# Query scales moved from the weights to the evictions, and one column tile size, in a four-layer cross-attention kernel

## The chip, the cores and the metric

The kernel runs on one core of one Trainium2 chip. The metric is device time in microseconds of one execution, the median of several runs. The time before is 1969.5 us (3 runs, 1969.37 to 1971.12).

## The reference

For each of 16 batches, queries x (100 x 256) pass through four cross-attention layers against one context (361 x 256); everything is float32. Cut to what matters:

```python
# layer 0: 16 heads of 16, layer norm of queries and of context, then a feed-forward part
qn, kn, vn = ln(x, ln1_g, ln1_b), ln(ctx, ln1_g, ln1_b), ln(ctx, ln1_g, ln1_b)
x = x + attention(qn @ wq + bq, kn @ wk + bk, vn @ wv + bv) @ wo + bo
x = x + gelu(ln(x, ln2_g, ln2_b) @ w1 + b1) @ w2 + b2
# layer 1: 16 heads of 64, RMS norm of queries, context as it is
x = x + attention((rms(x) * norm_w) @ wq, ctx @ wk, ctx @ wv) @ wo
# layer 2: 16 heads of 64, rotary embedding of q and k, mask, residual, layer norm behind
x = ln(x + attention(rope(x @ Wq), rope(ctx @ Wk), ctx @ Wv, mask) @ Wo, ln_gamma, ln_beta)
# layer 3: 16 heads of 16, layer norm of queries (gq, betaq) and of context (gkv, betakv)
x = x + attention(ln(x, gq, betaq) @ Wq + bq, ..., ...) @ Wo + bo
```

A norm with scale g and shift b ahead of a product can be written in two ways: (z*g + b) @ W + bias, or z @ (g*W) + (b @ W + bias), with z the normalized rows.

## The kernel before

**Staging.** All weights stay in SBUF, in 12 slabs of 1 MB each (128 x 2048). Slab 0 holds the four weights of layer 0, slab 11 those of layer 3; the others hold one weight each. One SP queue issues the transfers in a fixed chain: inputs of batch 0, column vectors, slab 0, constants, mask of batch 0, inputs of batch 1, row vectors, slabs 1 to 11. The raw context of a batch has one buffer (ctxr).

**Folding.** fold() (L487) takes a scale and a shift into weights. shift (L502) is a TensorE product of the weight with the shift, matmuls with one column of moving data; add_bias (L512) adds the bias and gives a column in `folded`; scale (L527) multiplies the rows of the weight on VectorE or GpSimd. For values, the bias goes on through the output weight into a row (L551, L557). Before the change this is done for wk, wq and wv of layer 0, for w1, and for Wq, Wk and Wv of layer 3; for wq of layer 1 only the scale.

**A batch.** keys_T transposes the context twice, raw (cT) and normalized (zT). queries_T (L650) transposes normalized queries z by four TensorE transposes (L664) into two PSUM banks, and each bank is copied to xT by ScalarE or VectorE (copied, L604 and L606). It is called five times per batch, three times for normalized queries with a folded scale and shift (layer 0, feed-forward, layer 3). project_T and on_columns (L708) do the projections. Attention works in units of four heads: scores (L815), for layer 2 the mask (L860), the maximum (L863), exp (L866), reciprocal (L838), division by the sum on GpSimd (L845), transposes of the probabilities (L899), their copies (pT), and the weighted values (L935). Residuals run through project_out and project_out_T (L1007).

**Tile modes.** TensorE's array is used in tiles. Scores of 64 rows and transposes are "row64", scores of 16-wide heads are "row32", projections take column tiles of 64 ("col64") or 32 ("col32"), whichever is set (ANY_COLUMNS). Weighted values take col64 for heads of 64 and col32 for heads of 16. The folding has no mode (None).

**Order.** Nothing is issued in the order in which the program is written. Each piece of work goes into a Plan with its engines, expected costs, buffers and mode. Plan.order (L208) simulates the engines and picks the next piece: among those whose inputs and buffers are given, the one that starts first, then that of lowest rank. The rank comes from the batch, the length of the chain behind the piece, and ORDER's numbers for each batch ("batch", "lag") and each place in a batch ("place"). Leaving a tile mode counts as late by "keep" nanoseconds until the mode has run for "run". "pull" counts work of the other mode that is at hand:

```python
if engine == "PE" and start < free_at["PE"] + ORDER["window"]:
    m = mode if set_now else w.modes[0]
    at_hand[m] = at_hand.get(m, 0.0) + busy
```

Buffers named with p = b % 2 are separate for even and odd batches, so about two batches are in work at a time.

Of the kernel before, what the change touches and what calls it, by code (L numbers as in the profile page):

```python
# [17 lines left out]
P = 128  # L18
# [13 lines left out]
for _name, _w in (  # L32
# [12 lines left out]
    ("L0_xattn_wq", "L0_xattn_wk", "L0_xattn_wv", "L0_xattn_wo"),  # L45
# [10 lines left out]
    "lag": 38400, "pull": 0.05, "window": 0,  # L56
    "keep": {None: 890, "row64": 230, "row32": 260, "col64": 340, "col32": 1300},
    "run": {None: 2660, "row64": 8610, "row32": 9590, "col64": 0, "col32": 580},
    "batch": (-18000, 5000, 3000, 2500, 0, -3500, -2000, -500, 4000, 500, -500, -1500, -1500, 1500, 2000, -30500),
    "place": [  # L60
        100 * k for k in (
        -449, 380, -410, -907, -297, -381, -841, -547, -865, -451, -58, -715, -384, -1275, -204,
        -641, 28, -182, 1370, -396, -764, -381, 852, -627, -112, 190, -9, -445, -3, -270, -165,
        -33, -304, -1025, -413, 303, 189, 748, 664, 428, 334, -443, 389, -680, 26, 45, -389,
        -703, -298, -815, 382, 144, -234, -178, -319, -57, -490, 535, -270, -557, 24, 37, -252,
        -893, -744, -709, -7, -615, -499, -843, -1740, -583, -894, -541, 9, -686, -216, -11,
        -752, 14, -65, -104, -468, 267, 152, -304, 178, -1193, -774, -328, -678, -328, 230, 62,
        -355, -400, -649, -377, -283, 67, -55, 958, -172, 913, 10, -206, -336, -713, -315, -919,
        -196, -1027, -1062, 110, -555, 199, -65, 638, -159, -330, -421, -1032, -459, -215, -509,
        -581, 677, -93, -54, -2, -397, -37, -164, 39, -112, 653, -319, -353, 304, -753, -267,  # L70
        -601, -483, -215, 631, -145, -379, -439, -89, -73, -773, 104, -225, 235, -417, 26, -258,
        13, -847, -1259, -285, -870, 806, -187, -611, 97, 247, -582, -680, 50, -1341, -248, -93,
        -616, -282, -235, -362, -155, 207, 94, 84, 80, -312, 78, -97, -754, -266, 199, -192,
        -730, -101, -622, -421, -44, 28, 272, 825, 35, 688, -974, -421, 99, -655, -589, -47,
        -596, -713, -247, -457, -229, 16, -8, -207, 57, 717, 105, -410, -430, -320, -80, -938,
        -425, -769, -201, -686, -203, -784, -115, -998, -715, -1135, -1148, -736, -659, -883,
        -423, -884, -340, -196, -208, -45, 21, -200, -443, -268, 144, -548, -442, 252, -63, 450,
        0, 579, -46, 20, 860, 146, -344, -813, -172, -250, 576, -43, -365, -496, -37, -48, 63,
        -524, 157, -854, 1077, 547, -55, 635, -106, 360, -340, 719, -224, -240, -384, 434, 98,
        -620, -34, 307, 467, 169, -533, -297, 357, -181, 345, 49, -249, -145, 132, 86, -613,  # L80
        -65, -229, -858, 50, 445, -116, 64, -92, 11, 52, 185, 242, 201, 148, -390, -231, -174,
        -101, 39, -360, -62, 745, 81, 97, -526, -14, 324, -4, 136, 120, 442, -331, 163, -56,
        -176, -297, 608, 379, 66, -125, 660, 278, 251, -61, 531, 319, 711, 828, -180, -66, 279,
        -14, -193, -319, -511, -66, -29, 83, 113, 31, -672, -659, -715, -95, -394, -632, 260,
        -250, 170, -179, -139, -14, 37, -407, -1281, -867, -1330, -1460, -919, -876, -673,
        -2528, -934, -1119, -766, -1231, -576, -595, -612, -708, -115, 489, 492, 25, 2, 709,
        682, 185, 91, 381, -723, 578, 713, 883, -107, 47, -29, 470, -264, -587, 294, -539, 205,
        511, 423, 312, 1194, 30, 288, 344, -534, 37, -29, -165, -729, -641, -757, -867, -180,
        -1043, -773, -2062, -647, -1793, -1205, -894, -1713, -2979, -1137, 480, -214, -732,
        -916, -495, -1134, 349, -519, 213, -1447, -683, 961, -1008, -1158, -424, -1113, -152,  # L90
        -394, -88, 120, -537, 445, -938, 43, -331, -1264, -1001, -589, -634, -395, -837, -386,
        -399, -199, -576, -704, -569, -1503, -1874, -612, -1400, 35, -689, 192, 101, -184, 648,
        -1555, 146, -563, -45, -17, -467, -239, 338, -101, -408, 321, 31, 300, 37, -514, -472,
        131, -1083, -709, 337, -131, -233, -1021, -499, -1152, -521, -555, -660, 1181, -1469,
        -901, -1632, -540, -1293, 38, 0, 355, 184, 358, 379, 123, -235, -102, 603, -537, -68,
        -207, 39, -451, -373, 620, 695, 238, -360, 624, -675, -500, -309, 228, -1657, -1006,
        -1864, -2116, -1377, -1805, -1217, -2242, -2683, -3027,
# [208 lines left out]
def tile_xattn_layers(  # L306
# [112 lines left out]
    def load_slab(i):  # L419
        t = const.tile([P, 2048], F32, name=f"slab{i}")  # L420
        b = load_const(t, slabs[i], 2.6, f"slab{i}")
        names = SLABS[i]
        n = len(names)
        for k, name in enumerate(names):
            part = t[:, k * (2048 // n) : (k + 1) * (2048 // n)]
            kc = 8 if n == 1 and name[-2:].lower() in ("wo", "w2") else 2
            w[name] = part.rearrange("p (c n) -> p c n", c=kc)
            slab_of[name] = b
# [11 lines left out]
    load_slab(0)  # L440
    cst_b = load_const(cst, consts, 1.0, "cst")
    plan.batch = 0
    masks[0] = load_mask(0)
    plan.batch = 1
    loads[1] = load_inputs(1, 1000.0, 5000.0)
    plan.batch = -1
    rows_b = load_const(rows, rowvecs.partition_broadcast(P), 1.7, "rows")
    for i in range(1, len(SLABS)):
        load_slab(i)
# [34 lines left out]
    folded = const.tile([P, 7, 8], F32, name="folded")  # L484
    fold_at, ready_w = {}, {}

    def fold(slab_names, g, b, outs):  # L487

        src = slab_of[slab_names[0]]
# [28 lines left out]
        if biased:  # L518
            n = sum(w[o[0]].shape[2] // P for o in biased)
            plan.add(on_pe((1, 4 * n)), shift, reads=[src, colt_b], writes=[ps])  # L520
            plan.add(on_dve(8, len(biased)), add_bias, reads=[ps, colt_b], writes=[fb])
        for name, _, out_bias in outs:
            ready_w[name] = plan.buf(None, f"ready_{name}")

            def scale(eng, name=name):
# [7 lines left out]
                on_dve(n, 2) + on_pool(2 * n * 1.5), scale, reads=[src, fb, colt_b],  # L533
# [3 lines left out]
            if out_bias is not None:  # L537
# [22 lines left out]
                plan.add(on_pe((E, 4)), through, reads=[wide, src], writes=[rps])  # L560
# [9 lines left out]
        [("L0_xattn_wk", "L0_xattn_bk", None), ("L0_xattn_wq", "L0_xattn_bq", None),  # L570
# [3 lines left out]
    def fold_later():  # L574
        fold_b["ff"] = fold(
            SLABS[1], "L0_xattn_ln2_g", "L0_xattn_ln2_b", [("L0_xattn_w1", "L0_xattn_b1", None)]
        )
        fold(SLABS[3], "L1_xattn_norm_w", None, [("L1_xattn_wq", None, None)])

        fold_b["3q"] = fold(  # L580
            SLABS[11], "L3_xattn_gq", "L3_xattn_betaq", [("L3_xattn_Wq", "L3_xattn_bq", None)]
        )
        fold_b["3k"] = fold(
# [63 lines left out]
    def whole(a):  # L647
        return a

    def queries_T(src, p, name, cls="xT"):  # L650


        t = plan.buf(f"{cls}{p}", name)
# [718 lines left out]
```

## Time and profile before

| | |
|---|---|
| median of 3 runs | 1969.5 us |
| profiled execution | 1972.8 us, span 1971.0 us |
| mean granted TensorE clock | 0.991 |
| TensorE busy | 1932.3 us, 98% |
| VectorE, ScalarE, GpSimd busy | 1383.9, 1113.1, 954.6 us |
| TensorE matmul instructions | 30809 |
| one-column matmuls of the folding (L502) | 80 instructions, 13.2 us busy |
| period of one batch in the steady state | 119.5 us |

A float32 matmul of the program is two matmul instructions in the trace, each with its weight load. A shape such as 128*64 128x512 is rows * columns of the tile, then the moving data. Busy times of TensorE overlap, since matmuls are pipelined and tiles run side by side; the time from the start of one group to the start of the next is the time that the group costs. A batch's period is read from groups that come back in the same order.

### The profile page before, as it was taken

What the parts mean: (1) busy time and instruction counts of PE and PEld (TensorE: products, weight loads), DVE (VectorE), ACT (ScalarE), POOL (GpSimd) and SP (SyncE); (2) the same over time, 40 slices, a digit from 0 to 9 for tenths busy, and PEclk for the clock granted to TensorE, in tenths of its full rate; (3) what the DMA queues carried; (4) which work ended last, traced back from release to release, by engine and by line L of the source; (5) the groups of instructions that cost most, each with busy time, mean ns of one, the idle gap of its engine ahead of it and who ended that gap; (6) DMA issues with size and microseconds to landing.
All of it is one profiled execution on the core that took longest, in us unless ns stands there. A gap on an engine that the chain in (4) does not pass through costs nothing.

```text
span 1971.0 us, 72999 instructions
## 1 busy us (share of the span) xinstructions
PE 1932.3 (98%) x30809; PEld 1310.7 (66%) x30809; DVE 1383.9 (70%) x3781; ACT 1113.1 (56%) x3330; POOL 954.6 (48%) x1524
## 2 busy tenths in 40 slices
PE   7999999999999999999999999999999999999997
PEld 5667666676766767666676666767667676666666
DVE  4547676767777667776777777667776677767576
ACT  2546566555565655556565665555656555565545
POOL 3344554545455454454545545454554545544454
PEclk8999999999999999999999999999999999999997
DMA  7000000000000000000000000000000000000000
GB/s 295 6 2 13 4 9 6 4 13 4 11 7 2 13 4 11 7 2 13 5 13 5 11 4 5 13 5 11 6 2 13 4 11 6 3 13 5 2 2 6
DMA packets 14479, 28.23 MB, mean 14 GB/s; under 512 B 3346, under 2 KB 12360, under 8 KB 12616
## 3 DMA queue, kind: packets, MB, share of 16 engines
q1 hardware_dynamic: 14152, 23.56, 3.7%
q8 instruction: 242, 3.96, 0.8%
q14 instruction: 85, 0.70, 0.1%
HBM read 21.92 MB, written 1.64 MB: 12 GB/s over the span
## 4 chain that ended last, share of the span: by engine, by line
PE 80%; DVE 9%; POOL 5%; ACT 3%; issue 2%; DMA 0%; POOLq 0%; SPq 0%; ACTq 0%; DVEq 0%
PE ps L708 48%; PE ps L815 12%; PE ps L935 9%; PE ps L899 9%; POOL prob L845 3%; ACT prob L866 2%; DVE two L863 2%; DVE ctxr L1257 1%; POOL kT L776 1%; DVE ps L860 1%; DVE rot L1288 1%; PE ps L664 1%; DVE z L640 1%; DVE pT L606 1%; POOL sw L768 1%
## 5 line engine op out<-in xcount | busy, mean ns | idle before, releaser
L845 POOL TENSOR_SCALAR prob<-prob,two 100x361 f32<-100x361 f32 x1024 | 573.1, 576 | 689.6 <-DVE two L838 604.4
L866 ACT ACTIVATE prob<-ps,two 100x361 f32<-100x361 f32 x1024 | 568.5, 568 | 206.5 <-DVE two L863 180.3
L863 DVE TENSOR_REDUCE two<-ps 100x1 f32<-100x361 f32 x1024 | 491.2, 524 | 153.9 <-PE ps L815 152.1
L708 PE MATMUL ps<-slab,cT 128*64 128x512 f32 (+1 forms) x2008 | 363.7, 596 | 0.0
L708 PE MATMUL ps<-cT,slab 128*64 128x361 f32 (+1 forms) x2640 | 346.6, 468 | 0.1
L604 ACT COPY pT<-ps 128x384 f32<-128x384 f32 (+1 forms) x511 | 232.8, 496 | 155.2 <-PE ps L899 114.3
L815 PE MATMUL ps<-kT,qT 32*100 32x181 f32 (+3 forms) x4096 | 301.4, 328 | 0.0
L815 PEld LDWEIGHTS ps<-kT,qT 32*100 32x100 f32 (+1 forms) x4096 | 229.3, 165 | 68.0 <-issue 25.1
L899 PEld LDWEIGHTS ps<-ident,prob 64*128 64x128 f32 (+1 forms) x6144 | 218.7, 139 | 79.8 <-issue 38.2
L899 PE MATMUL ps<-ident,prob 36*128 36x36 f32 (+1 forms) x6144 | 249.1, 227 | 2.3 <-POOL prob L845 2.0
L708 PEld LDWEIGHTS ps<-cT,slab 128*64 128x64 f32 (+1 forms) x2640 | 132.7, 124 | 121.7 <-issue 113.7
L866 ACT ACTIVATION_READ_ACCUMULATOR prob<-ps,two 100x1 f32 x1024 | 211.9, 207 | 0.0
L606 DVE COPY pT<-ps 128x432 f32<-128x432 f32 (+1 forms) x257 | 146.4, 577 | 81.2 <-PE ps L899 79.2
L708 PEld LDWEIGHTS ps<-slab,cT 128*64 128x64 f32 (+1 forms) x2008 | 95.4, 121 | 135.2 <-issue 124.2
L768 POOL TENSOR_TENSOR sw<-sw,rot 128x361 f32<-128x361 f32 x128 | 105.5, 824 | 147.9 <-DVE sw L764 84.0
L935 PEld LDWEIGHTS ps<-pT,v 128*64 128x64 f32 (+1 forms) x3072 | 138.9, 136 | 33.6 <-issue 23.7
L935 PE MATMUL ps<-pT,v 128*64 128x100 f32 (+1 forms) x3072 | 155.7, 251 | 0.0
L860 DVE TENSOR_TENSOR ps<-ps,cap 100x361 f32<-100x361 f32 x256 | 130.6, 533 | 20.0 <-PE ps L815 10.6
L604 ACT COPY v<-ps 128x512 f32<-128x512 f32 (+1 forms) x133 | 78.0, 587 | 113.4 <-PE ps L708 112.4
L708 PEld LDWEIGHTS ps<-xT,slab 128*64 128x64 f32 (+1 forms) x2624 | 116.9, 137 | 24.8 <-issue 14.3
L838 DVE RECIPROCAL two<-two 100x2 f32<-100x2 f32 x512 | 78.4, 159 | 72.2 <-ACT prob L866 70.4
L776 POOL TENSOR_TENSOR kT<-kT,sw 128x361 f32<-128x361 f32 x128 | 122.3, 956 | 12.2 <-DVE kT L771 6.9
(97 smaller groups left out, 2189.5 us busy)
## 6 DMA issues: line engine op xcount, KB each, us to landing
slab<-slabs_dram SPq DMA_DIRECT2D x12, 1024.0 KB
ctxr<-ctx_dram SPq DMA_DIRECT2D x16, 256.0 KB
ctxr<-ctx_dram SPq DMA_DIRECT2D x16, 105.0 KB
x<-x_dram SPq DMA_DIRECT2D x16, 100.0 KB
out_dram<-x SPq DMA_DIRECT2D x16, 100.0 KB
mask<-mask_dram SPq DMA_DIRECT2D x16, 45.1 KB
rows<-rowvecs_dram SPq DMA_DIRECT2D x1, 640.0 KB
cst<-consts_dram SPq DMA_DIRECT2D x1, 362.0 KB
```

Source lines behind the costliest of these rows:

```text
L604: nc.scalar.copy(dst(), src())
L606: nc.vector.tensor_copy(dst(), src())
L708: nc.tensor.matmul(out_f(t, t1), lhsT=lhsT[:, t:t1], rhs=rhs, start=start, stop=stop, tile_position=(0, t),)
L768: nc.gpsimd.tensor_tensor(a, a, wide(sin()), ALU.mult)
L776: nc.gpsimd.tensor_tensor(dst_f(dst.ap), dst_f(dst.ap), sw.ap[:, :n], ALU.add)
L815: nc.tensor.matmul(banks[h].ap[:S, k0:k1], lhsT=self.q_of(h), rhs=self.k_of(h)[:, k0:k1], start=(k0 == 0), stop=(k1 == SK), skip_group_che ...
L845: nc.gpsimd.tensor_scalar(p.ap[:S, :SK], p.ap[:S, :SK], rsum.ap[:S, j : j + 1], 1.0, ALU.mult, ALU.mult,)
L860: nc.vector.tensor_tensor(s(), s(), self.cap.ap[:S, :], ALU.min)
L863: nc.vector.tensor_reduce(neg_max.ap[:S, 0:1], s(), AX.X, ALU.max, negate=True)
L866: nc.scalar.activation(prob.ap[:S, :SK], s(), AF.Exp, bias=neg_max.ap[:S, 0:1], accum_out=sums.ap[:S, j : j + 1],)
L899: nc.tensor.transpose(out[:, c, :], probs[h].ap[q0:q1, c * KP : (c + 1) * KP], ident[q0:q1, q0:q1],)
L935: nc.tensor.matmul(ps.ap[t * w0 : (t + 1) * w0, cols], lhsT=lhsT, rhs=pTs[h][0].ap[:n, pTs[h][1], c, :], start=(c == 0), stop=(c == NKC - ...
```

## The change

It has four parts.

- Scales and shifts of queries: wq of layer 0, w1 and Wq of layer 3 are no longer folded. queries_T takes the names of a scale and a shift (`affine`), and each bank is evicted in two pieces (one for each half of the 256 features), by an activation with scale and bias, or by a tensor_scalar that multiplies and adds. The plain biases bq and b1 are used in place of `folded`.
- Column work: on_columns always uses tiles of 32; the weighted values of 64-wide heads too, as two tiles of 32 for each head. All of it is mode "col32".
- Transfers: slab 0 is ordered wk, wv, wq, wo and comes in two transfers of 512 KB, each with its own dependency; row vectors and slab 1 are issued ahead of the inputs of batch 1.
- ORDER has new numbers throughout. A batch has more pieces of work than before, so "place" has more entries.

```diff
-    ("L0_xattn_wq", "L0_xattn_wk", "L0_xattn_wv", "L0_xattn_wo"),
+    ("L0_xattn_wk", "L0_xattn_wv", "L0_xattn_wq", "L0_xattn_wo"),
...
-    "lag": 38400, "pull": 0.05, "window": 0,
-    "keep": {None: 890, "row64": 230, "row32": 260, "col64": 340, "col32": 1300},
-    "run": {None: 2660, "row64": 8610, "row32": 9590, "col64": 0, "col32": 580},
-    "batch": (-18000, 5000, 3000, 2500, 0, -3500, -2000, -500, 4000, 500, -500, -1500, -1500, 1500, 2000, -30500),
+    "lag": 78500, "pull": 0.15, "window": 0,
+    "keep": {None: 260, "row64": 220, "row32": 1340, "col64": 2740, "col32": 2110},
+    "run": {None: 2810, "row64": 13010, "row32": 14900, "col64": 44290, "col32": 780},
+    "batch": (-373500, -1500, 0, 0, 0, 0, 0, 0, 0, 0, 0, 0, 0, 0, -500, -101500),
...
-    load_slab(0)
+    load_slab(0, 2)
     cst_b = load_const(cst, consts, 1.0, "cst")
+    rows_b = load_const(rows, rowvecs.partition_broadcast(P), 1.7, "rows")
     plan.batch = 0
     masks[0] = load_mask(0)
+    plan.batch = -1
+    load_slab(1)
     plan.batch = 1
     loads[1] = load_inputs(1, 1000.0, 5000.0)
     plan.batch = -1
-    rows_b = load_const(rows, rowvecs.partition_broadcast(P), 1.7, "rows")
-    for i in range(1, len(SLABS)):
+    for i in range(2, len(SLABS)):
         load_slab(i)
...
-        [("L0_xattn_wk", "L0_xattn_bk", None), ("L0_xattn_wq", "L0_xattn_bq", None),
+        [("L0_xattn_wk", "L0_xattn_bk", None),
          ("L0_xattn_wv", "L0_xattn_bv", ("L0_xattn_wo", "L0_xattn_bo"))],
...
-        fold_b["ff"] = fold(
-            SLABS[1], "L0_xattn_ln2_g", "L0_xattn_ln2_b", [("L0_xattn_w1", "L0_xattn_b1", None)]
-        )
...
-        fold_b["3q"] = fold(
-            SLABS[11], "L3_xattn_gq", "L3_xattn_betaq", [("L3_xattn_Wq", "L3_xattn_bq", None)]
-        )
...
+            for c in range(2):
+
+                def scaled(eng, i=i, c=c, q0=q0, q1=q1):
+                    g, shift = (col(k, c) for k in affine)
+                    out, src = t.ap[:, c, q0:q1], tp(i)[:, c, :]
+                    if eng == "ACT":
+                        nc.scalar.activation(out, src, AF.Identity, bias=shift, scale=g)
+                    else:
+                        nc.vector.tensor_scalar(out, src, g, shift, ALU.mult, ALU.add)
+
+                plan.add(
+                    on_act(q1 - q0 + 100) + on_dve(q1 - q0 + 60), scaled,
+                    reads=[banks[i], colt_b], writes=[t],
+                )
...
-    def on_columns(mode, out_f, lhsT, rhs, start, stop):
+    def on_columns(out_f, lhsT, rhs, start, stop, at=0):
-        width = int(mode[3:])
         n = lhsT.shape[1]
-        for t in range(0, n, width):
-            t1 = min(t + width, n)
+        for t in range(0, n, 32):
+            t1 = min(t + 32, n)
...
-                            w0 = max(hd, 32)
-                            nc.tensor.matmul(
-                                ps.ap[t * w0 : (t + 1) * w0, cols], lhsT=lhsT,
-                                rhs=pTs[h][0].ap[:n, pTs[h][1], c, :], start=(c == 0),
-                                stop=(c == NKC - 1),
-                                tile_position=(0, t * w0),
+                            on_columns(
+                                lambda r0, r1: ps.ap[r0:r1, cols], lhsT,
+                                pTs[h][0].ap[:n, pTs[h][1], c, :], c == 0, c == NKC - 1,
+                                t * max(hd, 32),
                             )
...
-                mode=f"col{max(hd, 32)}",
+                mode="col32",
...
-            mode=ANY_COLUMNS,
+            mode="col32",
```

## Prediction

> **What bounds the kernel now.** I read the share of each engine first, then TensorE's waits, then its timeline (start-to-start times give the real cost of a group; a printed duration includes the pipeline's end), then the stretches at both ends, and last the queue of SP.
>
> ```profile
> PE 1932.3 (98%) x30809; PEld 1310.7 (66%) x30809; DVE 1383.9 (70%) x3781; ACT 1113.1 (56%) x3330; POOL 954.6 (48%) x1524
> 590.00:709.50 119.50, 118.33 (x1918) 80.18 (x1920) 86.57 (x237) 69.14 (x207) 58.99 (x93) 1.00 0.03 8
> PE ps L664 <- DVE z L640: 10.0, 15, 1.3
> PE ps L690 <- DVE rT L1007: 7.1, 13, 0.6
> PE ps L470 <- DMA crow<-colvecs_dram: 5.5, 1, 5.5
> PE ps L502 <- DMA slab<-slabs_dram: 3.4, 1, 3.4
> ```
>
> The first line is the page's: PE 98%, the next engine 70%. The second is one period of the steady state (one batch, 119.5 us): PE is idle 1.17 us of it. All its idle time is in a handful of waits, 17 us of them behind z and rT over 15 batches. So TensorE sets the time, and a change counts by what it does to TensorE's stream: work, switches of tile mode, idle gaps, and clock.
>
> ```profile
> 9.83 5.25 PE L502 MATMUL ps<-colt,slab 128*128 128x1 f32 x24 [3.39 <-DMA slab<-slabs_dram]
> ...
> 16.95 5.08 PE L708 MATMUL ps<-zT,slab 128*64 128x361 f32 x16 [0.83 <-ACT xT L604]
> ...
> 27.22 5.15 PE L502 MATMUL ps<-colt,slab 128*128 128x1 f32 x32
> 32.30 1.54 PE L815 MATMUL ps<-kT,qT 32*100 32x181 f32 x16
> ...
> 30.00:40.00 10.00, 9.26 (x72) 6.92 (x73) 4.36 (x8) 3.36 (x12) 2.70 (x2) 0.52 1.02 426
> ...
> 507.09 1.94 PE L708 MATMUL ps<-slab,cT 128*64 128x512 f32 x8
> 508.86 1.38 PE L708 MATMUL ps<-cT,slab 128*64 128x361 f32 x8
> 510.17 0.34 PE L664 MATMUL ps<-ident,z 64*128 64x64 f32 x4
> ...
> 569.25 3.62 PE L708 MATMUL ps<-slab,cT 128*32 128x512 f32 x32
> 572.80 0.87 PE L815 MATMUL ps<-kT,qT 32*100 32x181 f32 x16
> ```
>
> L502 is the folding of shifts into biases: matmuls with one column. They take 5 us each time in the head. The stretch from 30 to 40 us has a granted clock of 0.52 (the column after the five engines). The last five timeline rows are the prices of tile sizes: 8 matmul instructions of 64 columns against 32 of 32, and the step into a row group (L664, L815). SP's own timeline shows its queue standing for 11 us:
>
> ```profile
> 4.04 0.43 SPq L404 DMA_DIRECT2D mask<-mask_dram  x1
> 15.74 0.38 SPq L386 DMA_DIRECT2D ctxr<-ctx_dram  x1
> 16.21 0.42 SPq L390 DMA_DIRECT2D ctxr<-ctx_dram  x1
> 16.69 0.33 SPq L391 DMA_DIRECT2D x<-x_dram  x1
> 17.06 0.35 SPq L414 DMA_DIRECT2D rows<-rowvecs_dram  x1
> 17.46 14.31 SPq L414 DMA_DIRECT2D slab<-slabs_dram  x11
> ```
>
> **What the Trainium skill says.** "TensorE: Matmul & The Clock Gate", in "The HAM clock gate", says that TensorE runs at half clock until a window of about 3.4 us was busy, and falls back after an idle one; in "PE-mode transpose", that transposes don't count as busy. The trace agrees: 16 key matmuls from 16.95 us take 4.84 us to the next start, and 2.43 us in the steady state; clock 0.52 follows the 32 one-column matmuls. That one-column matmuls count as nearly idle is my inference. "TensorEngine Tiling (Array Packing)", in "Key Properties", says that a change of tiling mode drains TensorE: here it costs 0.11 us (below). The clock page's "Wait — 56ns, not 53.3ns?" gives a floor of about 25 ns between starts; here 24 matmuls of 128*32 with 100 columns (L935) take 0.54 us, 22.5 ns each with four column tiles side by side, so the measurement decides and halving the tiles isn't excluded by issue.
>
> **Part 1: the folding leaves the queries and the first feed-forward weight.** Of 40 folding products (2 instructions each, 80 in the trace) 24 go: wq 4, w1 16, Wq 4. Where they stand: 8 instructions at 216 ns in the group at 9.83 (5.18 us to the next start, by 24), all 32 at 27.22 (5.08 us to the next start), 8 in a third group of 24 that takes 2.84 us, 118 ns each. Sum 1.73 + 5.08 + 0.94 = 7.75 us of TensorE, all on the path. The clock: behind those 32, L815 x16 took 1.47 us to its next start instead of 0.80, and the transposes, keys and queries up to 39.4 us lose about 2.7 us by the same comparison; together 3.4 us. I take it as gained; ends 0 (something else idles the window) and 5. The column scaling of these weights by DVE and POOL (L527, 9.9 us in all) lay beside TensorE: nothing.
>
> **Part 2: what comes instead.** queries_T with a scale and shift issues four evictions of 64 or 36 columns in place of two of 128 and 72, in 48 calls: 192 for 96. By L1073 (DVE, two pointer operands, 128x100) 375 ns, against 249 for a plain copy of that size; on ACT a pointer costs 561 - 463 = 98 ns (L1034 against the copy of 361 columns; the skill's "ScalarE: Activation LUTs" says about 93). So about 340 to 420 ns each, 192 x 0.38 = 73 us for 96 x 0.25 = 24 us: 49 us more over DVE and ACT together, 2% of their 2497 us. Neither becomes the bound. The chain z to xT lengthens by 0.3 to 0.5 us per call; other matmuls cover it (waits at L708 for xT are 1.8 us in the whole run). Cost 0; if the cover is gone 48 x 0.4 = 19 us, and behind TensorE's in-order queue everything waits.
>
> **Part 3: slabs and the transfer queue.** SP issues the load of batch 1 at 15.74 us, because the only ctxr slot is free only then; rows and 11 slabs queue behind it (DMA share 0.26 from 10 to 20 us, 1.00 after). The change issues rows and slab 1 ahead (1.66 MB, 4.3 us at 388 GB/s), into that gap: batch 1's load loses nothing if they are done by 15 us, the later slabs come some 4 us earlier, mask 0 waits without a reader. The first half of slab 0 lands 512 KB earlier, 1.3 us (0 if both halves share the engines evenly): 1.3 us off L502's wait of 3.4. One more DMA issue of 0.4 us on SP, covered.
>
> **Part 4: tiles of 32.** About 12,900 matmul instructions of 64 columns become twice as many, with their weight loads. By start-to-start medians in the steady state: 512 columns, 8 of 64 take 1.76 us, 16 of 32 take 1.72 (the two rows above: 3.55 for 32 with one switch of 0.11); 361 columns 1.22 and 1.21; 256 columns 0.91 and 0.86 behind a boundary, 0.86 both inside a group; 100 columns 2.75 for x64 and 2.75 for x128; weighted (L935) 1.09 for 24 and 2 x 0.54. Per batch 7 x 0.04 + 15 x 0.01 = 0.43 us less, x16 = 7; I take 6, ends 0 and 9.
>
> **Part 5: switches of mode.** 512-column groups take 1.87 us before a row64 group and 1.76 before the same mode; 361-column groups 1.32 and 1.22: a switch costs 0.11 us. I counted 47 per period in the timeline: 22 times from rows to columns (16 to col64, 6 to col32), 22 back, 3 between row modes; 5.2 us of 119.5. Only 3 in the whole run go between col64 and col32, so the merge removes few directly; but work of both kinds can now share a stretch of columns, and order() keeps columns for at least 780 ns where col64 was left at once ("run" was 0). `pull` does nothing: with "window" 0 no start lies before free_at. I take 5 fewer per period: 5 x 0.11 x 15 = 8 us; ends +12 per period (20 us lost) and -12 (20 us gained). The new ranks are not to be read by eye.
>
> **Part 6: ends and gaps.** Waits in the steady state are 17 us, the last 71 us hold about 11 idle and some at half clock. Batch 15 now starts with rank offset -101500 for -30500, so it lies more beside batch 14. I take -4 us, ends +8 and -15.
>
> **Sum.** -7.8 - 3.4 - 1.3 - 6 - 8 - 4 = -30.5 us. The profiled execution took 1972.8 us (span 1971.0), 3.3 over the median 1969.5. 1972.8 - 30.5 = 1942.3, as a median 1939.
>
> **The rivals.** *A, only the head gains*: the xT chain is exposed by the new order and the switches stay: -12.5 - 6 + up to 19 for the chain, so between no change and -18; about 1955. For it: z waits are already the largest. Against: each is 0.67 us, and other work is at hand. *B, the order gains more*: 12 fewer switches per period (-20) and the tail -15: 12.5 + 6 + 35 = 53 us less, 1916. *C, slower, by switches*: if the new order alternates more between rows and columns, each extra switch per period costs 0.11 x 15 = 1.65 us; the other parts bring 12.5 + 6 + 4 = 22.5, so from 14 more per period (61 for 47) it gives a loss; at 20 more, 33 - 22.5 = 10 slower, 1980. For it: row32 may now hold its mode for 1340 ns. Against: one mode fewer to alternate between. *D, no difference*: the chain's 19 us meet the gains of the head and tiles, 1969.
>
> **Chances.** The forecast 0.55, A 0.18, B 0.11, C 0.11, D 0.05. The range 1912 to 1964 reaches over A's centre and takes in B's. Measured differences under 0.2% (4 us) can't be told from none. Faster 0.84, same 0.05, slower 0.11.
>
> **What would show it.** TensorE's instructions near 43,900; L502 x32 for x80; clock near 1.0 from 30 to 40 us; the period at about 118 us with some 42 switches; waits for xT under 5 us. A period over 119.5 us, or waits at L708 for xT in tens of us, would prove me wrong.

## The result, and the profile after

The median went from 1969.88 us to 1969.05 us (12 runs of each). The ratio is 0.9995, with a 95% interval from 0.9986 to 1.0004: no difference that can be told. The forecast was 1939 us, and its range ended at 1964. The profiled execution took 1969.54 us (span 1967.7), 3.3 us less span than before; it was forecast at 1942.3.

From the page of the changed kernel, the engines and the queue that brings instructions (before: 242 packets, 3.96 MB):

```profile
PE 1918.1 (97%) x43881; PEld 1270.8 (65%) x43881; DVE 1389.0 (71%) x3802; ACT 1135.7 (58%) x3398; POOL 959.6 (49%) x1522
...
q8 instruction: 345, 5.65, 1.2%
```

TensorE has 14 us less busy time and 13,072 more matmul instructions. Yet the span is only 3.3 us shorter, so TensorE now idles 11 us more. The windows of the same kernel: three single periods, and the stretch where the clock was 0.52. Behind a stretch and its length stand the busy times of PE, PEld, DVE, ACT and POOL, then the clock:

```profile
574.58:694.11 119.53, 117.95 (x2744) 77.93 (x2740) 86.85 (x238) 70.88 (x212) 59.50 (x94) 1.00 0.03 8
694.11:814.00 119.89, 118.31 (x2744) 78.05 (x2740) 86.94 (x238) 70.65 (x212) 59.53 (x94) 1.00 0.04 9
1173.95:1294.76 120.81, 118.87 (x2745) 78.78 (x2742) 86.78 (x238) 70.76 (x212) 59.56 (x94) 1.00 0.03 8
30.00:40.00 10.00, 10.00 (x192) 5.39 (x185) 4.78 (x12) 5.14 (x14) 1.75 (x3) 1.00 1.01 420
```

Two things are new. The periods are uneven: the same 2744 or 2745 matmuls take 119.53, 119.89 or 120.81 us. The 13 periods from 213.72 to 1775.50 us have a mean of 120.14, against 119.55 before, where they lie between 119.52 and 119.63. And the shortest is no shorter than a period before: it has 0.38 us less busy time (117.95 for 118.33) and 0.41 us more idle time (1.58 for 1.17). The clock from 30 to 40 us is 1.00; the trace still has one stretch of 3.4 us at half clock just ahead of it, from 26.4 to 29.8 us (before: 10.2 us, from 29.3 to 39.5).

TensorE's waits, in us, with the number of times and the longest:

```profile
PE ps L915 <- POOL prob L861: 10.9, 18, 1.5
PE ps L666 <- DVE z L642: 9.8, 15, 1.4
PE ps L708 <- ACT prob L882: 5.9, 13, 0.5
...
PE ps L725 <- DMA slab<-slabs_dram: 2.5, 1, 2.5
PE ps L725 <- issue: 2.1, 5, 0.7
...
PE ps L511 <- DMA slab<-slabs_dram: 1.8, 1, 1.8
```

The wait for z is as it was. The wait behind VectorE's rT (7.1 us) is gone but for 0.3 us. In its place stand L915, the transposes of the probabilities, behind GpSimd's division, and L708 behind the exp on ScalarE. "issue" is a wait for nothing that the profile shows. In TensorE's timeline the folding and the new wait for a slab:

```profile
8.12 3.54 PE L511 MATMUL ps<-colt,slab 128*128 128x1 f32 x16 [1.85 <-DMA slab<-slabs_dram]
...
26.35 4.31 PE L725 MATMUL ps<-cT,slab 128*32 128x361 f32 x32 [2.54 <-DMA slab<-slabs_dram]
```

**Where the time went.** I compared the start of the k-th group of scores (of 256) in both kernels. After minus before is -10.8 us at the 32nd, -8.3 at the 112th, -5.5 at the 176th and -3.3 at the end. So the head did gain 11 us, and the rest of the run gave 7.5 back, in steps.

### The profile page after: what moved, and what is told of

Same layout as the page of the kernel before. It is cut to its first block, busy times and chain, and to the rows that moved or that the text cites. A ratio compares the mean times of both kernels' runs of the same rounds, so it can differ in the third digit from the quotient of the medians.

```text
span 1967.7 us, 99209 instructions
## 1 busy us (share of the span) xinstructions
PE 1918.1 (97%) x43881; PEld 1270.8 (65%) x43881; DVE 1389.0 (71%) x3802; ACT 1135.7 (58%) x3398; POOL 959.6 (49%) x1522
## 4 chain that ended last, share of the span: by engine, by line
PE 82%; DVE 11%; POOL 3%; issue 1%; ACT 1%; DMA 1%; SPq 0%; ACTq 0%; POOLq 0%; DVEq 0%
PE ps L725 58%; PE ps L831 12%; PE ps L915 10%; POOL prob L861 2%; DVE two L879 2%; DVE ps L876 1%; DVE rot L1302 1%; POOL sw L784 1%; DVE mv L620 1%; DVE ctxr L1271 1%; PE ps L666 1%; DVE sw L780 1%; ACT prob L882 1%; DMA slab<-slabs_dram 1%; DVE z L642 1%
## 5 line engine op out<-in xcount | busy, mean ns | idle before, releaser
L725 PE MATMUL ps<-slab,cT 128*32 128x512 f32 (+1 forms) x3072 | 363.4, 595 | 0.0
L725 PE MATMUL ps<-cT,slab 128*32 128x361 f32 x4096 | 359.2, 470 | 2.9 <-DMA slab<-slabs_dram 2.5
L915 PEld LDWEIGHTS ps<-ident,prob 36*128 36x128 f32 (+1 forms) x6144 | 215.4, 139 | 89.1 <-POOL prob L861 42.3
L915 PE MATMUL ps<-ident,prob 64*128 64x64 f32 (+1 forms) x6144 | 239.5, 227 | 11.0 <-POOL prob L861 10.9
L725 PEld LDWEIGHTS ps<-cT,slab 128*32 128x32 f32 x4096 | 126.3, 109 | 117.9 <-issue 104.3
L608 DVE COPY pT<-ps 128x384 f32<-128x384 f32 (+1 forms) x246 | 134.1, 570 | 64.2 <-PE ps L915 51.5
L725 PE MATMUL ps<-pT,v 128*32 128x100 f32 (+1 forms) x6144 | 159.2, 250 | 2.2 <-DVE pT L608 1.2
L725 PEld LDWEIGHTS ps<-pT,v 128*32 128x32 f32 (+1 forms) x6144 | 137.7, 110 | 36.0 <-issue 27.4
L876 DVE TENSOR_TENSOR ps<-ps,cap 100x361 f32<-100x361 f32 x256 | 125.0, 532 | 22.5 <-PE ps L831 21.7
L725 PEld LDWEIGHTS ps<-xT,slab 128*32 128x32 f32 x5120 | 115.5, 111 | 21.3 <-issue 16.2
L725 PE MATMUL ps<-xT,slab 128*32 128x100 f32 x5120 | 126.2, 252 | 2.8 <-issue 1.8
```

Source lines behind the costliest of these rows:

```text
L608: nc.vector.tensor_copy(dst(), src())
L725: nc.tensor.matmul(out_f(at + t, at + t1), lhsT=lhsT[:, t:t1], rhs=rhs, start=start, stop=stop, tile_position=(0, at + t),)
L876: nc.vector.tensor_tensor(s(), s(), self.cap.ap[:S, :], ALU.min)
L915: nc.tensor.transpose(out[:, c, :], probs[h].ap[q0:q1, c * KP : (c + 1) * KP], ident[q0:q1, q0:q1],)
```

## The experiments

Kernels a_... are the changed kernel with an edit, kernels b_... the kernel before with an edit. Intervals are those of the ratio to the kernel before.

### Is it the tiles of 32?

**a_wide**: the changed kernel in its own order, but each stretch of column work uses tiles of 64, unless it holds weighted values of 16-wide heads.

```diff
-        for t in range(0, n, 32):
-            t1 = min(t + 32, n)
+        for t in range(0, n, width):
+            t1 = min(t + width, n)
...
+            kinds = {o.kind for o in pe_work[i:j]}     # one contiguous stretch of col32
+            for o in pe_work[i:j]:
+                width_of[o.index] = 32 if "narrow" in kinds else 64
```

> The changed kernel with its order kept to the instruction; only the tile width differs: every stretch of columns without weighted values of 16-wide heads is issued in tiles of 64, as before the change. Theory S (instruction supply): the tiles of 32 double TensorE's instructions, and in stretches of 100-column matmuls they are used up faster than they come, which costs irregular stalls, on average 0.6 us over the shortest period of 119.53 us, 8 us in all. S expects about 1961 us, and periods as even as before the change. Rival O (the new order's own waits, 1.6 us per period before GpSimd's, ScalarE's and VectorE's results, set the loss): 1969 us, periods still uneven. Rival W (tiles of 32 are the faster ones, as I forecast): 1975 us.

Measured: 1964.27 us, ratio 0.9971 (0.9961 to 0.9981), with 30,801 matmul instructions. The periods are even again: twelve from 119.57 to 119.66 and one of 119.94, mean 119.64. So in this order tiles of 32 cost 5 us, and the unevenness is theirs.

**a_short32**: as a_wide, but a stretch that holds any work with 100 columns of moving data stays at 32.

```diff
-                width_of[o.index] = 32 if "narrow" in kinds else 64
+                width_of[o.index] = 32 if kinds & {"narrow", "short"} else 64
```

> The changed kernel in its own order; tiles of 64 only in stretches of columns that hold no 100-column matmuls, tiles of 32 in all others. Theory S, if the dense 100-column stretches are what outruns the supply: stalls stay, 1967 to 1969 us. If instead the number of instructions over a whole period counts: about half way to the other variant, 1965 us. Rival O: 1969 us. Rival W: 1971 us.

Measured: 1968.16 us, 0.9995 (0.9988 to 1.0001), periods from 119.53 to 120.73. It undoes less than it seems to, since nearly every stretch holds some short work: only 872 instructions go (43,009 left). It shows that the remaining 43,009 are enough for the whole loss, and no more.

**b_32**: the kernel before in its own order, with nothing changed but all column work in tiles of 32.

```diff
-        width = int(mode[3:])
+        width = 32
...
-                            nc.tensor.matmul(
-                                ps.ap[t * w0 : (t + 1) * w0, cols], lhsT=lhsT,
...
+                            for r0 in range(0, w0, 32):
+                                at = t * w0 + r0
...
```

> The kernel before the change, its order kept, with all column work issued in tiles of 32 (the plan still books col64). Theory S: the even period of 119.54 us becomes uneven and 0.4 to 0.8 us longer, 1976 to 1980 us in all. Rival O: no change, 1969.5 us. Rival W: 0.43 us per period less, 1963 us.

Measured: 1971.10 us, 1.0007 (0.9999 to 1.0015): no difference from before that can be told, and less than theory S expected. Three of its 13 periods are long; two usual ones and one of the long:

```profile
460.37:579.73 119.36, 118.17 (x2747) 78.32 (x2744) 86.63 (x236) 69.08 (x207) 59.02 (x94) 1.00 0.03 8
579.73:699.11 119.38, 118.18 (x2746) 78.30 (x2744) 86.59 (x237) 69.07 (x207) 59.04 (x94) 1.00 0.03 9
...
1057.28:1177.70 120.42, 118.38 (x2746) 78.36 (x2744) 86.58 (x236) 69.06 (x207) 59.03 (x94) 1.00 0.03 8
```

This is Part 4 by itself. Where nothing stalls, tiles of 32 save 0.16 us per period (119.37, the mean of the two usual rows, for 119.53, the median before), not 0.43. And some periods lose about 1 us, in this order too.

### What stalls: a measurement by itself

**b_probe**: behind the last batch of the kernel before, 512 matmuls in tiles of 64 and then 1024 in tiles of 32, 100 columns each. They are the same products from the same operands; nothing reads them and TensorE waits for no other engine.

```diff
+        for width, count in ((64, 512), (32, 1024)):
+            for k in range(count):
+                t0 = k * width % P
+                nc.tensor.matmul(
+                    slots["ps"][k * width // P % 8][t0 : t0 + width, :S],
+                    lhsT=w["L1_xattn_wq"][:, 0, t0 : t0 + width],
+                    rhs=slots["cT"][0][:, 0, :S], start=True, stop=True, tile_position=(0, t0),
+                )
```

> The kernel before the change with two blocks of extra matmuls behind its last work, results unused: 512 matmuls of tiles of 64 with 100 columns (1024 instructions and as many weight loads), then 1024 matmuls of tiles of 32 with 100 columns (2048 and 2048). Both blocks are the same array work, 43 ns x 1024 = 21.5 ns x 2048 = 44 us at full clock. Theory S: TensorE's instruction queue is refilled in packets of 256 instructions that start no less than about 3.4 us apart, 13 ns per instruction, so the second block runs at first at 21.5 ns per matmul instruction and then at about 26.6, 50 to 55 us in all; the first block stays at 43 ns. If the supply is no limit: 44 us each. If stalls come from input transfers that meet the instruction transfers, there are none here (no input is loaded at the end): 44 us each.

TensorE's timeline (start, duration, tile, count, idle time before it):

```profile
1965.95 50.11 PE L1326 MATMUL ps<-cT,slab 128*64 128x100 f32 x1288
2016.49 2.95 PE L1326 MATMUL ps<-cT,slab 128*32 128x100 f32 x128 [0.43 <-issue]
2019.96 2.95 PE L1326 MATMUL ps<-cT,slab 128*32 128x100 f32 x128 [0.52 <-issue]
2023.71 2.95 PE L1326 MATMUL ps<-cT,slab 128*32 128x100 f32 x128 [0.80 <-issue]
```

The first row has all 1024 instructions of 64 columns and the first 264 of 32, with no gap: 1024 x 43 ns + 264 x 22 ns are 49.8 of its 50.1 us (43 and 22 are 2.75 us by 64 and by 128, the start-to-start times that the prediction used). From then on TensorE stops after every 128 matmuls (this is one execution, traced once). 128 matmuls with their weight loads are 256 instructions, and so are the packets: this kernel has 266 packets on the instruction queue for 242 before, 24 more for 6144 more instructions of TensorE. A block of 256 comes every 3.66 us on average (13 from 2016.49 to 2064.11 us), 14.3 ns per instruction, and TensorE runs it in 2.75 us. The trace also has the start of each packet on that queue: each of the 14 rows from 2016.49 us on begins 2.3 to 2.9 us after the start of one packet of its own (2014.07 for 2016.49, 2017.60 for 2019.96, 2021.10 for 2023.71). So the tiles of 32 ran at full speed only as long as a store of instructions lasted, and then at the speed of supply. The 264 matmuls are not the size of that store, since packets came meanwhile. By its own row a stretch of 128 looks free, and that is the row that I priced from.

### Is it the same stall in the kernel?

The longest period of the changed kernel (1173.95 to 1294.76 us) loses its time in one place. The timeline there, with a few rows left out:

```profile
1240.06 2.93 PE L725 MATMUL ps<-xT,slab 128*32 128x100 f32 x128
1242.80 1.46 PE L725 MATMUL ps<-pT,v 128*32 128x100 f32 x46
...
1247.64 1.24 PE L725 MATMUL ps<-pT,v 128*32 128x100 f32 x48
1248.70 0.47 PE L725 MATMUL ps<-cT,slab 128*32 128x361 f32 x1
1249.53 1.11 PE L725 MATMUL ps<-cT,slab 128*32 128x361 f32 x12 [0.35 <-issue]
...
1250.52 3.21 PE L725 MATMUL ps<-oT,slab 128*32 128x100 f32 x124
...
1254.96 0.32 PE L708 MATMUL ps<-ident,rT 64*100 64x64 f32 x4
...
640.68 2.95 PE L725 MATMUL ps<-xT,slab 128*32 128x100 f32 x128
...
650.23 2.93 PE L725 MATMUL ps<-oT,slab 128*32 128x100 f32 x128
...
654.31 0.32 PE L708 MATMUL ps<-ident,rT 64*100 64x64 f32 x4
```

The last three rows are the same work in the shortest period. From the 128 matmuls of xT to the transposes of rT it takes 14.90 us in the one and 13.63 in the other: 1.27 us, the whole difference of the two periods. The profile calls 0.35 us of it a wait; the rest is in groups that only take longer, such as one 361-column matmul with 0.83 us to the next start. So the 2.1 us of "issue" in the table of waits are the visible part of the loss. It is the same place in all 13 periods: this stretch takes 13.63 to 14.91 us, and what is left of the period always 105.88 to 105.97 us, but for one of 106.25.

The packets tie it to the supply. The wait at 1249.53 us ends 2.43 us after a packet started (at 1247.10), and the other four waits for "issue" end 2.60 to 2.65 us after one, as in b_probe. Each of these packets came late: it started 6.1 to 9.2 us after the one before it, where b_probe has 3.4 to 4.0.

This stretch is dense: 440 matmuls and their weight loads in 13.63 us, 15.5 ns per instruction, where the whole period has 21.8. That is just slower than the 14.3 of b_probe's supply, but within it the 128 matmuls of xT and the 128 of oT take 2.75 us each, 10.7 ns per instruction.

**a_dense64**: the changed kernel, with tiles of 64 only in stretches of columns with more than 3200 ns of planned work of 100 columns (over 150 matmul instructions).

```diff
+                width_of[o.index] = 64 if "narrow" not in kinds and sum(
+                    x.engines[0][1] for x in pe_work[i:j] if x.kind == "short") > 3200 else 32
```

> The changed kernel in its own order; tiles of 64 only in the stretches of columns with more than 150 matmul instructions of 100 columns and no 16-wide heads (about 3 of 23 per period), 32 everywhere else. Theory S, density: nearly all stalls go with these few stretches, periods even at 119.5 to 119.7 us, 1961 to 1964 us in all, as with tiles of 64 nearly everywhere. If the total of instructions counts and not the density: stalls stay, 1967 us. Rival O: 1969 us.

Measured: 1962.64 us, 0.9956 (0.9944 to 0.9968). Two successive periods:

```profile
452.94:572.40 119.46, 117.94 (x2416) 78.17 (x2412) 86.85 (x238) 70.66 (x212) 59.35 (x94) 1.00 0.03 8
572.40:691.89 119.49, 117.95 (x2416) 78.21 (x2413) 86.81 (x238) 70.79 (x212) 59.37 (x94) 1.00 0.03 8
```

Eleven of the 13 periods lie between 119.47 and 119.55, the other two are 119.67 and 119.84; the mean is 119.54, and there is no "issue" among the waits. 38,625 matmul instructions are left, 88% of the changed kernel's, and the loss is gone: it is the crowding of instructions that costs, not their number. (To take as many instructions out of other stretches was not tried; a_short32 took 872 out of those and kept the loss.) The interval lies wholly below that of the change itself. Against before, the k-th scores stand at -11.1 us early in the run and -10.8 at the end: the head's gain is now kept.

### The head, the transfers and the scaled evictions

Three kernels keep the order of before, with the folding of wq, w1 and Wq planned but not issued. **b_head** has the scaled evictions and the moved transfers; **b_plain** the moved transfers and plain copies, which leaves out the scales and shifts of the queries; **b_unfold** plain copies and the transfers as before.

```diff
+    UNFOLDED = ("L0_xattn_wq", "L0_xattn_w1", "L3_xattn_Wq")
...
+                if name in UNFOLDED:
+                    continue
...
+            def scaled(eng, i=i, q0=q0, q1=q1):        # b_head alone
+                for c in range(2):
...
+            if name == "cst":                          # b_head and b_plain
+                early["rows"](None)
+            elif name == "rows":
+                early["slab1"](None)
```

> The kernel before the change, its order and tile widths kept, with the scales and shifts of queries in the evictions (wq, w1 and Wq not folded, both halves of a bank evicted by one piece of work) and the first slab in two transfers, rows and slab 1 issued ahead. If the head's gain is real and independent of the order: 11 us less, 1958 us, with periods of 119.5 us. If the longer evictions are exposed in an order that was not made for them: up to 0.4 us per call in 48 calls, so between 1958 and 1977 us. If the head's gain needs the new order: 1965 to 1969 us.

> The kernel before the change in its order and tile widths, with the folding of wq, w1 and Wq left out, plain copies of the queries as before (so scales and shifts of those queries are left out), and the transfers of the change. Beside the variant that also has the scaled evictions (1975 us, period 120.0 us, inputs of batch 2 transposed 7.4 us earlier) it tells head from evictions. If the evictions made its loss: period back at 119.54 us and 7 to 9 us less than before, 1961 to 1963 us. If the moved transfers made it: about 1972 to 1975 us.

> The kernel before the change in its order, tile widths and transfers; only the folding of wq, w1 and Wq is left out, queries are evicted by plain copies (scales and shifts of those queries are left out). Beside the variant that has the moved transfers too (1965.3 us, inputs of batch 2 transposed 6.9 us earlier than before): if the folding matmuls are the gain, as I forecast (7.75 us of TensorE and 3.4 us of clock of the 12.5): 1964 to 1967 us and 5 to 7 us earlier; if the transfers are: 1968 to 1970 us and 1 to 2 us earlier.

Measured: b_head 1975.34 us, 1.0032 (1.0019 to 1.0044), slower; b_plain 1965.29, 0.9967 (0.9953 to 0.9980); b_unfold 1965.90, 0.9976 (0.9967 to 0.9985).

b_unfold runs ahead of before by 6.9 us from about 100 us to the tail. The first fence shows the stretch that stood at clock 0.52, in b_unfold and then in b_plain; the second shows three waits in the head of b_unfold:

```profile
30.00:40.00 10.00, 7.66 (x66) 3.35 (x62) 4.64 (x14) 4.93 (x16) 5.94 (x9) 1.00 1.02 424
...
30.00:40.00 10.00, 10.00 (x72) 4.61 (x68) 4.71 (x14) 5.26 (x18) 3.53 (x7) 0.83 1.01 423
```

```profile
10.81 3.54 PE L506 MATMUL ps<-colt,slab 128*128 128x1 f32 x16 [4.46 <-DMA slab<-slabs_dram]
...
34.10 1.44 PE L730 MATMUL ps<-cT,slab 128*64 128x361 f32 x8 [2.00 <-DMA slab<-slabs_dram]
36.67 3.65 PE L730 MATMUL ps<-slab,cT 128*64 128x512 f32 x16 [0.34 <-DMA slab<-slabs_dram]
```

In b_unfold, without those one-column matmuls, the clock is full here. With them it was half for 10.2 us before, and for 6.8 in b_probe, whose head is the same; without them b_plain, b_head and the changed kernel still have 3.4 us at half (30.1 to 33.5, 28.4 to 31.8 and 26.4 to 29.8 us). So these matmuls held the clock down for most of the stretch, and something else in part of the kernels for one shorter piece; no run tells what (one execution of each was traced). That they held it down agrees with the Trainium skill, "TensorE: Matmul & The Clock Gate", in "The HAM clock gate", if such matmuls count as idle; the page doesn't say that they do. The forecast gave folding and clock 11.2 us. The waits for slabs grow by 1.07 us at L506 and 2.34 at L730, and 11.2 - 3.4 = 7.8 is near the 6.9 measured: TensorE is early, and the next slab isn't there. b_plain, with the slabs ahead, gains no more: its waits for slabs are gone, and 2.2 us behind VectorE's statistics (mv) and 2.2 behind a copy (ctxr) stand in their place, beside the 3.4 us at half clock.

b_head starts the same way (-7.4 us) and then loses 0.46 us in each of eleven periods (119.98 to 120.09, for 119.53) and 2.1 us in each of the other two. The lines show one of these two and a stretch in it, then the wait behind rT (7.1 us before; that behind z is 10.0 in both), then the rows around rT in a usual period of b_head and in one of b_plain:

```profile
457.84:579.45 121.61, 120.27 (x1922) 81.68 (x1920) 87.30 (x238) 70.67 (x211) 59.00 (x94) 0.99 0.03 8
519.89:523.30 3.41, 3.41 (x31) 2.91 (x29) 2.04 (x7) 0.90 (x2) 0.55 (x1) 0.50 0.00 0
...
PE ps L731 <- DVE rT L1048: 9.2, 13, 0.7
...
638.39 1.18 PE L940 MATMUL ps<-ident,prob 64*128 64x64 f32 x24
640.27 0.32 PE L731 MATMUL ps<-ident,rT 64*100 64x64 f32 x4 [0.71 <-DVE rT L1048]
...
635.78 0.96 PE L940 MATMUL ps<-ident,prob 64*128 64x64 f32 x24
637.28 0.32 PE L731 MATMUL ps<-ident,rT 64*100 64x64 f32 x4 [0.54 <-DVE rT L1048]
```

So the scaled evictions are not free. They cost 12.8 us between b_plain and b_head (0.9967 and 1.0032, the two intervals apart; the two profiled executions are 8.8 us apart), and hardly any of it is a wait for xT. Period against period, b_head is at most 0.1 us behind b_plain up to the transposes of the probabilities ahead of rT, and 0.46 us behind once those of rT start: from the one start to the other it takes 1.88 us for 1.50. The named wait for rT is 0.17 us of that; the rest lengthens the transposes themselves, which the table of waits doesn't count. That ScalarE and VectorE, with more work in the same order, hand over later there is my reading. In the two long periods the clock stood at 0.50 for 3.4 us right behind this place (519.9 to 523.3 and 881.7 to 885.1 us), which cost 1.6 us each; no other profiled kernel has that between 100 and 1900 us, and why it does is open.

**a_plain**: the changed kernel with plain copies in the place of the scaled evictions, which leaves out the scales and shifts of the queries. **a_plain64**: the same on a_dense64.

```diff
-                        nc.scalar.activation(out, src, AF.Identity, bias=shift, scale=g)
+                        nc.scalar.copy(out, src)
...
-                        nc.vector.tensor_scalar(out, src, g, shift, ALU.mult, ALU.add)
+                        nc.vector.tensor_copy(out, src)
```

> The changed kernel in its own order, with plain copies of the same pieces where queries_T applies scale and shift (the scales and shifts of queries of layers 0, feed-forward and 3 are left out). Tells what the pointer operands of the evictions cost in the new order. If the new order covers them (my prediction, cost 0): 1968 to 1969 us, shortest period 119.5 us. If the chain from z to xT is exposed (rival A): up to 0.2 us per call in 48 calls, so 1960 to 1964 us and a shortest period of about 119.0 us.

> The variant with tiles of 64 in the dense stretches alone (1962.6 us), with plain copies in place of the scaled evictions of queries (their scales and shifts are left out). Without the supply stalls it prices the pointer operands in the new order. If they are covered (my prediction): 1962.6 us, shortest period 119.46. If they are exposed as in the variant with stalls (shortest period 119.30 for 119.53): 0.23 us per period and something at both ends, 1957 to 1960 us.

Measured: a_plain 1962.80 us, 0.9959 (0.9948 to 0.9971), and a_plain64 1958.86, 0.9939 (0.9925 to 0.9953). Both keep the four pieces of each call, so they price the scale and the shift alone, where b_plain for b_head has two pieces for four as well. In the new order scale and shift cost 7 us with the stalls about (after 0.9995, a_plain 0.9959). Without the stalls they cost some 3 us (a_dense64 0.9956, a_plain64 0.9939; these two intervals overlap, and the periods tell them apart: 119.54 and 119.39 on average). The periods lose it in one wait, ahead of the transposes of rT, here in a_dense64 and in a_plain64:

```profile
PE ps L709 <- ACT prob L886: 5.5, 13, 0.4
...
PE ps L709 <- ACT prob L886: 3.1, 13, 0.2
```

It is a wait for an exp on ScalarE, the engine that runs 115 of the 192 scaled evictions. The price of one of these was right; the groups of the changed kernel (count, busy us, mean ns, idle before):

```profile
L686 ACT ACTIVATE xT<-ps,colt 128x64 f32<-128x64 f32 x66 | 25.7, 412 | 23.0 <-PE ps L666 23.0
...
L686 ACT ACTIVATE xT<-ps,colt 128x36 f32<-128x36 f32 x49 | 17.7, 389 | 0.1
```

The Trainium skill, "ScalarE: Activation LUTs", in "What ACT_TABLE_LOAD costs", gives 186 ns + 0.833 ns for each element and 93 ns for each pointer operand: 425 ns by estimate for 64 columns with a scale and a bias, 412 measured. The 77 on VectorE took 315 ns at the median, a little under the forecast.

### What waits in the steady state of the new order?

The changed kernel waits in each period first 0.46 us ahead of the transposes of rT (L708) and then 0.54 us ahead of those of the probabilities (L915):

```profile
875.08 0.32 PE L708 MATMUL ps<-ident,rT 64*100 64x64 f32 x4 [0.46 <-ACT prob L882]
875.93 1.71 PE L915 MATMUL ps<-ident,prob 64*128 64x64 f32 x48 [0.54 <-POOL prob L861]
```

The 48 matmuls are the transposes of probabilities 8 and 9 of layer 2, which GpSimd has just divided; 4 to 7 are older and are transposed later. **a_moved** (a_dense64 with an edit) takes 4 to 7 ahead of the transposes of rT. **a_moved2** takes them between rT and 8 and 9.

```diff
+        for b in range(1, B):
+            for tp in ("tp0", "tp1"):
+                at, k = place_of(f"ff_xt_{b}_ps0"), place_of(f"L2_{b - 1}_1_{tp}")        # a_moved
+                at, k = place_of(f"L2_{b - 1}_2_tp0"), place_of(f"L2_{b - 1}_1_{tp}")     # a_moved2
...
+                ordered.insert(at, ordered.pop(k))
```

> The variant with tiles of 64 in the dense stretches alone (1962.6 us), and one more edit: in each period the transposes of probabilities 4 to 7 of layer 2 (their divisions on GpSimd were done 4 us earlier) are issued ahead of the transposes of rT and of probabilities 8 and 9, which TensorE waits for (0.43 and 0.54 us per period). No switch is added, all of them are row64. If TensorE is the bound all through and these waits are the order's own loss (theory O for the part that isn't supply): up to 0.97 us per period, 13 us, so 1950 to 1953 us. If the waits only move on, because TensorE's later work waits for the same engines: 1960 to 1962 us.

> As the variant whose moved transposes made it slower (1971.9 us, period 120.3 us, waits for z of the RMS norm 0.75 us and for ScalarE 0.7 us), but the transposes of rT stay in front: order rT, probabilities 4 to 7, then 8 and 9. Tells why that one lost. If it lost because rT's rows were late and the chain rT, statistics, z, queries is what the next work waits for: the chain is early again here, and the 0.54 us of waiting for GpSimd goes, so up to 7 us below 1962.6: 1955 to 1959 us. If it lost because the transposes of 4 to 7 have to wait for PSUM banks that earlier exps still read: the waits move in front of them here too, 1963 to 1970 us.

Measured: a_moved 1971.94 us, 1.0008 (1.0000 to 1.0017), 0.5% behind a_dense64 and slower than either of my two expectations. Its periods take 120.25 to 120.69 us, and a new wait leads its table:

```profile
PE ps L667 <- DVE z L1290: 9.8, 13, 0.8
PE ps L667 <- DVE z L643: 9.6, 15, 1.4
```

L1290 is the RMS norm of layer 1. It needs the residual that the transposes of rT finish, so what stands ahead of rT makes this norm late, and the queries of layer 1 behind it.

a_moved2 took 1960.14 us, 0.9941 (0.9929 to 0.9953): by its median the fastest version that computes the whole reference, though its interval overlaps that of a_dense64. A period and the same place in its timeline:

```profile
570.46:689.75 119.29, 118.12 (x2417) 78.38 (x2413) 86.72 (x238) 70.66 (x212) 59.35 (x94) 1.00 0.03 8
```

```profile
870.61 0.32 PE L709 MATMUL ps<-ident,rT 64*100 64x64 f32 x4 [0.42 <-ACT prob L886]
870.74 0.24 PE L919 MATMUL ps<-ident,prob 64*128 64x64 f32 x1
871.14 1.81 PE L919 MATMUL ps<-ident,prob 36*128 36x36 f32 x47 [0.16 <-ACT prob L886]
```

GpSimd's 0.54 us is gone from the place, 0.16 stands there, and the idle time of the period is 1.17 us, what it was before the change. The periods average 119.39 us, 0.15 less than in a_dense64. So the 0.41 us that the new order idled more was this wait, in the main; less than half of it comes back as time, since the busy time rises (118.12 for 117.94).

## Why the prediction was wrong

**What bounds the kernel** was right: the time followed TensorE's stream in each run. But the list of what can delay that stream ("work, switches of tile mode, idle gaps, and clock") lacked a fifth thing, the supply of its instructions.

**Part 4, tiles of 32 (-6 us, ends 0 and 9), is the step that failed.** It had two faults. The gain was mis-sized: 0.16 us per period in b_32, not 0.43. I had taken medians of start-to-start times, some from groups at boundaries; which of them misled isn't tested. Worse, I closed the cost with "halving the tiles isn't excluded by issue", from 22.5 ns per matmul over 24 of them and 2.75 us over 128. Both runs are shorter than the 264 matmuls for which the store of instructions lasted in b_probe; from then on the same matmuls took 28.6 ns (3.66 us by 128). A step that adds over 40% more instructions to the engine that sets the time had no row of profile behind its sustained rate, and its lower end stood at 0. Measured: +0.61 us per period by the mean over the shortest period, 8 us in 13 periods. With the gain of 2 us that makes +6 for the -6 forecast, 12 of the 27 us by which the profiled execution missed.

**Part 5, switches (-8 us).** The price was right, 0.11 us. The number was a guess: by the same count there are 46 per period, not 42, for 47. The new order has no changes between row modes (3 before), and its stretches of columns are nearly as many as they were (23 for 22). One switch is worth 1.4 us in 13 periods.

**Part 2, evictions (0 us, end 19).** The price of one (340 to 420 ns) was right on ScalarE and the cover was not. I looked at the wait for xT alone and asked whether ScalarE or VectorE became the bound; neither did. The changed kernel has no wait of TensorE's matmuls for xT, as I said. Yet scale and shift cost 3 us without the stalls, mostly in a wait for an exp on ScalarE, and the evictions cost 13 us in the order of before, where the transposes around rT come later; about 3 of these, in the profiled execution, are the two stretches at half clock.

**Parts 1 and 3, the head (-12.5 us with the clock).** Right in size: -11 us, with 32 instructions left (L511, 16 at 8.1 us and 16 at 56.1), clock 1.00 from 30 to 40 us and 3.4 us of half clock ahead of it. The mechanism is right in part: in the order of before, folding and clock are worth only 6.9, as slabs are then late, and the moved transfers add nothing. The other 4 us came with the new order. Of these, 2.4 us are shorter waits for slabs (1.85 + 2.54 for 4.46 + 2.00 + 0.34 in b_unfold); no run separates the rest.

**Part 6, ends and gaps (-4 us).** The tail came out at +0.5 us, and the idle time of the shortest period rose by 0.41 us, 5 us in 13 periods, behind GpSimd. I had not asked what the new ranks put ahead of a late result.

**The sum as measured**: head -11.4 (the first of the 13 periods starts at 213.72 us for 225.14), the 13 periods +7.7 (120.14 for 119.55), tail +0.5: -3.2, and -3.3 in the profiled spans. In the 13 periods: busy time -0.38 x 13 = -4.9 (tiles 2.1 and a switch 1.4 of it), idle +5.3, stalls +7.9, and -0.6 because these three are counted from a period of 119.50. Rival D named the result and, for its cause, the chain of xT against head and tiles. The result is near; the cause is another, since there is no wait for xT and the stalls alone outweigh what the tiles gain. Of the signs, the instructions (43,881), the folding x32, the clock from 30 to 40 us and xT came as I wrote; the period (120.14 for 118) and the switches (46 for 42) showed the error.

**What stays open.** Why the same stretch stalls in one period and not in the next isn't settled: ahead of each named stall a packet came late, but why it did then and not in other periods the traces don't say, and no run moved the packets. What put b_head at half clock twice is open too.

## What to carry to other kernels

Before tiles are halved, count the instructions of the engine that sets the time, weight loads too, over the densest few microseconds, and compare that with a rate measured over many hundreds of them: a short burst runs from a store and proves nothing. Uneven periods of equal work, with hardly a named wait, are the sign of it in a profile; give only the crowded stretches larger tiles. When a gain at the head is followed by no gain at the end, compare the two traces group by group: the point from which the lead shrinks says which part to take apart.

## What was new of the hardware

- TensorE's instructions came in packets of 16 KB, 256 instructions each. Where TensorE had to wait for each packet, in b_probe, a block of 256 took 3.66 us on average (3.47 to 4.03), and began 2.3 to 2.9 us after its packet started. In the changed kernel's trace no two packets start less than 3.33 us apart, and 21 gaps are under 3.6 us; in a_wide one is. Float32 matmuls of 100 columns in tiles of 32 use up 256 instructions in 2.75 us.
- The stall is only partly shown: of 1.27 us in the longest period 0.35 us is called a wait.
- Column tiles of 64 and 32 had nearly the same throughput when instructions were at hand: 0.16 us in 119.5.
